# Embedding attention on one core: 68 row tiles move from ScalarE's queue to GpSimd's gathers, and the last nine steps stand in another order

## The chip, the core and the metric

The kernel runs on one core of a Trainium2 chip. A core has a matrix engine (TensorE, PE in the profile, with its weight loads shown apart as PEld), a vector engine (VectorE, DVE), an activation engine (ScalarE, ACT), a programmable engine (GpSimd, POOL) and a queue engine (SyncE, SP). The engines run side by side and wait for each other by semaphores. The metric is the device time of one execution in microseconds (us); before the change the median of three runs is 11062.63 us, between 11062.41 and 11062.69.

## What is computed

For each of 16384 users, 69 rows of a table of 100001 rows of 96 floats are fetched, and one more row, q, for the label. Each of the 69 rows is weighed by a small network that sees it beside q; ten windows sum the weighed rows; a last network of three layers turns the sums and q into one number. Cut to what matters:

```python
u = emb[batch_user]                      # 16384 x 69 x 96
ql = emb[batch_label[:, 0]]              # 16384 x 96
z = concatenate([q, u, q - u, q * u], axis=-1)
h = dice(z @ W1 + b1, a1)                # 64 wide
att = (h @ W2 + b2) @ W3 + b3
pre = where(batch_user < ITEM_NUM, u * att, 0.0)
pooled = einsum('gf,bfe->bge', window, pre)
x = concatenate([pooled, ql], axis=-1)
h = dice(bn(x @ Wf1 + bf1), af1)         # 200 wide
h = dice(bn(h @ Wf2 + bf2), af2)         # 80 wide
out = h @ Wf3 + bf3
# dice(x, a) = (a * (1 - p) + p) * x, with p = sigmoid(x)
```

## The kernel before

**Tiles.** The users are cut into 32 blocks of 512. A chunk is one of the 69 fields of one block: 512 rows of the table, in four tiles of 128 rows, one row to a partition. There are 32 x 69 = 2208 chunks, numbered c, and so 8832 tiles. Two chunks make a step, so there are 1104 steps, numbered i from 0 to 1103.

**How a tile arrives.** Nearly all tiles come by a gather (L256): one GpSimd instruction with 128 row numbers, which fetches 128 rows. 132 tiles come in another way, always the last of a chunk's four. Their rows are fetched one by one into a ring of eight buffers by plain DMAs, 128 to a tile (L294). Of these tiles 64 are fetched by SyncE's queue (`SP_CHUNKS`, one in every 17 steps) and 68 by ScalarE's (`ACT_CHUNKS`, one in every 16 steps, eight rows in each step below 1088). For these tiles there is no gather, and PE waits for the ring's semaphore in its place (`wait_for_single`).

**A step.** `fetch(i)` issues the gathers of step i and, on PE, the eight transposes (L318) that put the rows into columns; VectorE copies each chunk's 96 x 512 out (uT, L369) and makes its product with q (quT, L370). Two steps later `hidden` multiplies both by the weights of the first layer (ph, L377 and L379) and ScalarE takes the sigmoid (y, L381); `gate` finishes the dice with ScalarE (L386) and VectorE (L387). One step later `attend` makes the weight of each row (pa, L394) and VectorE multiplies the rows by it (pre, L396). One more step later `top1` multiplies the weighed rows of both chunks by the first layer of the last network, with the window sum folded into its weights V, and adds into two accumulators of 100 x 512 (p1, L407), which gather over all 69 fields of a block.

**The end of a block.** When a block's last field is in, `top1_gates`, `top2` and `top3` finish it (L415 to L447), spread over the next steps. The last block has nothing behind it. There the old kernel leaves its steady order for the last six steps (`CLOSE = 6`): each part follows the step before it more closely, and then `top1_gates`, `top2` and `top3_last` run one after the other on whole 512 columns. `store` writes the first 31 blocks' results, `top3_last` the last block's.

**What sets the order.** The program is put down by hand: a plan lists for each step what is to be recorded, and each engine runs its own instructions strictly in the order in which they were recorded. PE and VectorE do all their work in one line each, GpSimd nothing but gathers after the first microseconds.

Of the kernel before, what the change touches and what calls it, by code (L numbers as in the profile page):

```python
# [23 lines left out]
DH = D1 // 2  # L24

BLK = 512
NBLK = B // BLK
NQ = BLK // P
NT = F * NQ
NCOL = NT + NQ  # L30
NPAIR = NBLK * F // 2
S_DICE = float(1.0 / np.sqrt(1.0 + 1e-9))
S_BN = float(1.0 / np.sqrt(1.0 + 1e-5))
# [3 lines left out]

NUT, NQUT = 8, 6

CLOSE = 6  # L40

NV = 4
PER_BANK = 512 // F
# [8 lines left out]
ACT_ROWS = 8  # L52
ACT_FIRST = 4
ACT_GROUP = 3
ACT_AHEAD = 5
ACT_CHUNKS = [2 * ((s + 1) * P // ACT_ROWS + ACT_AHEAD) for s in range(68)]
ACT_RING = 4
SINGLES = SP_CHUNKS + ACT_CHUNKS
NSB = (len(SINGLES) + P - 1) // P
# [4 lines left out]
def chunk_of(c):  # L64
    return divmod(c, F)
# [49 lines left out]
def rec_kernel(  # L115
# [13 lines left out]
    nc = tc.nc  # L129
# [5 lines left out]
    ypool = ctx.enter_context(tc.tile_pool(name="ypool", bufs=3))  # L135
    ppool = ctx.enter_context(tc.tile_pool(name="ppool", bufs=6))
    bpool = ctx.enter_context(tc.tile_pool(name="bpool", bufs=2))
    xpool = ctx.enter_context(tc.tile_pool(name="xpool", bufs=1))
# [46 lines left out]
    for i in range(2):  # L185
        t = const.tile([E + 1, BLK], F32, name=f"qT{i}")
# [18 lines left out]
    wf2 = FAR.of(wf, "Wf2").rearrange("e (k n) -> e k n", n=D2)  # L205
    wf3 = FAR.of(wf, "Wf3")
    bf1c = [FAR.of(wf, "bf1")[:, i : i + 1] for i in range(2)]
    af1c = [FAR.of(wf, "af1")[:, i : i + 1] for i in range(2)]
    bf2c = FAR.of(wf, "bf2")
    af2c = FAR.of(wf, "af2")  # L210
    bf3c = FAR.of(wf, "bf3")
    res = const.tile([P, NBLK * NQ], F32, name="res")

    def dice_weights(b, a, name):

        sb, sa, sna = (const.tile(list(b.shape), F32, name=f"{name}_{k}") for k in range(3))
# [17 lines left out]
    ps_h = ctx.enter_context(tc.tile_pool(name="ps_h", bufs=2, space=PSUM))  # L234
    ps_x = ctx.enter_context(tc.tile_pool(name="ps_x", bufs=2, space=PSUM))
# [3 lines left out]
    V = const.tile([E, F, D1], F32, name="V")  # L239
# [23 lines left out]
    def call(f, *args):  # L263
        return lambda: f(*args)
# [3 lines left out]
    class Singles:  # L268
# [19 lines left out]
        def fetch(self, s, start, stop):  # L288

            b, k = self.buffers[s % len(self.buffers)], s % NSEM  # L290
            for r in range(start, stop):
                if r % self.group == 0:
                    self.load(s, r)
                d = self.engine.dma_start(  # L294
                    out=ring[r : r + 1, b], in_=row_bytes[:, bass.ds(self.values[r], ROW_BYTES)]
                ).then_inc(self.sems[k], 16)
                tc.no_tile_sem_insts.add(d.ins.name)
                tc.declare_no_dep(d.ins, group=f"ring{b}", reason="a buffer's readers have waited for its rows")
                fresh.setdefault(b, []).append(d.ins)
            if stop == P:  # L300
                for ins in fresh.pop(b):
                    tc.add_to_no_dep_group(f"ring{b}", ins)
                self.given[k] += 16 * P
                places[self.chunks[s]] = b, self.sems[k], self.given[k]
# [3 lines left out]
    def single(c, t):  # L308
        return places.get(c) if t == SLOT else None
# [41 lines left out]
            if k < m  # L351
        ]

    def fetch(i, between=None):

        u = upool.tile([P, 8, E], F32, tag="u", name=f"u{i}")
        for j in range(2):
            if j == 1 and between:
                between()
            c = 2 * i + j  # L360
            n, k = chunk_of(c)
            ptr = ps_tr.tile([E, BLK], F32, tag="tr", name=f"ptr{c}")
            for t in range(NQ):
                if single(c, t):
                    wait_for_single(c, t)
                else:
                    gather(rows, u[:, 4 * j + t, :], ids[n][:, 4 * k + t : 4 * k + t + 1])
                read_rows(nc.tensor.transpose, ptr[:, t * P : (t + 1) * P], u, c, t, ident)
            nc.vector.tensor_copy(uTs[c % NUT][0:E], ptr)  # L369
            nc.vector.tensor_tensor(quTs[c % NQUT][0:E], ptr, qTs[n % 2][0:E], ALU.mult)  # L370
# [27 lines left out]
    def top1(c):  # L398

        n, k = chunk_of(c)  # L400
        if k == 0:
            p1s[n] = [ps_p.tile([DH, BLK], F32, tag=f"p{h}", name=f"p1_{n}_{h}") for h in range(2)]
            for h, p in enumerate(p1s[n]):
                nc.tensor.matmul(p, wq[:, h * DH : (h + 1) * DH], qTs[n % 2][0:E], start=True, stop=False)  # L404
        pre = pres.pop(c)
        for h, p in enumerate(p1s[n]):
            nc.tensor.matmul(p, V[:, k, h * DH : (h + 1) * DH], pre, start=False, stop=(k == F - 1))  # L407

    def top1_gates(n):

        x1s[n] = xpool.tile([DH, 2, BLK], F32, tag="x1", name=f"x1_{n}")
        gs = [xpool.tile([DH, BLK], F32, tag=f"g{h}", name=f"g1_{n}_{h}") for h in range(2)]

        def first(h):
            nc.scalar.activation(gs[h], p1s[n][h], AF.Sigmoid, bias=dice1[h][0], scale=S_BN * S_DICE)  # L415

        def second(h):
            _, sa, sna = dice1[h]
            nc.scalar.activation(gs[h], gs[h], AF.Identity, bias=sa, scale=sna)
            nc.vector.scalar_tensor_tensor(x1s[n][:, h, :], p1s[n][h], bf1c[h], gs[h], ALU.add, ALU.mult)  # L420

        return [call(f, h) for f in (first, second) for h in range(2)]

    def top2(n):
        x2 = xpool.tile([D2, BLK], F32, tag="x2", name=f"x2_{n}")
        g2 = xpool.tile([DH, BLK], F32, tag="g0", name=f"g2_{n}")[0:D2]
        p2 = ps_x.tile([D2, BLK], F32, tag="x", name=f"p2_{n}")
        for i in range(2):
            nc.tensor.matmul(p2, wf2[:, i, :], x1s[n][:, i, :], start=(i == 0), stop=(i == 1))  # L429
        x2s[n] = x2  # L430
        sb, sa, sna = dice2

        def first():
            nc.scalar.activation(g2, p2, AF.Sigmoid, bias=sb, scale=S_BN * S_DICE)  # L434

        def second():
            nc.scalar.activation(g2, g2, AF.Identity, bias=sa, scale=sna)  # L437
            nc.vector.scalar_tensor_tensor(x2, p2, bf2c, g2, ALU.add, ALU.mult)  # L438

        return [first, second]  # L440
# [13 lines left out]
        nc.vector.tensor_copy(r, p4)  # L454
        nc.sync.dma_start(out=out[n0 * P : n1 * P].rearrange("(m p) o -> m (p o)", p=P), in_=r)

    def top3_last(n):
        x2 = x2s.pop(n)
        p3 = ps_x.tile([1, BLK], F32, tag="x", name="p3_last")
        nc.tensor.matmul(p3, wf3, x2, start=True, stop=True)  # L460
        r = ypool.tile([P, BLK], F32, tag="y", name="r_last")[0:1]
        nc.vector.tensor_scalar(r, p3, bf3c[0:1], None, ALU.add)
        nc.sync.dma_start(out=out[n * BLK :].rearrange("p o -> o p"), in_=r)

    pres, p1s, x1s, x2s, qs, phs, ys = ({} for _ in range(7))
# [3 lines left out]
    def at(step, *work):  # L469
        plan.setdefault(step, []).extend(work)  # L470

    by_sync = Singles("sp", nc.sync, mybir.EngineType.SP, SP_CHUNKS, 0, range(SP_RING), 32)
    for s, m in enumerate(SP_CHUNKS):
# [5 lines left out]
        mybir.EngineType.Activation,  # L479
        ACT_CHUNKS,  # L480
        len(SP_CHUNKS),
# [11 lines left out]

    c = NPAIR - CLOSE
    last = NPAIR - 1
# [3 lines left out]
    def tops(step, chunks):  # L499
        for m in chunks:  # L500
            at(step, call(top1, m))
            n, k = chunk_of(m)
            if k == F - 1:
                gates[step], tops2[step + 1], tops3[step + 2] = n, n, n
# [43 lines left out]
    def both(k):  # L548
        return [2 * k, 2 * k + 1]

    at(c, call(hide, c - 2), call(attends, c - 3))
    tops(c, late + both(c - 4))
    at(c, call(fetch, c, call(hide, c - 1)))
    at(c + 1, call(attends, c - 2))
    tops(c + 1, both(c - 3))
    at(c + 1, call(attends, c - 1))
    tops(c + 1, both(c - 2))
    at(c + 1, call(fetch, c + 1, call(hide, c)))
    for i in range(c + 2, NPAIR):
        tops(i, both(i - 3))  # L560
        at(i, call(attends, i - 2), call(fetch, i, call(hide, i - 1)))
    i = NPAIR
    tops(i, both(i - 3))
    at(i, call(hide, last), call(attends, i - 2))
    tops(i, both(i - 2))
    at(i, call(store, 0, (NBLK - 1) * NQ), call(attends, last))
    tops(i, both(last))

    def finish():
        n = NBLK - 1  # L570
        for job in top1_gates(n):
            job()
        for job in top2(n):
            job()
        top3_last(n)

    at(i, finish)

    for n in range(NBLK):
        first = n * F // 2  # L580
# [86 lines left out]
```

## Time and profile before

| | us |
|---|---|
| median of three runs | 11062.63 |
| the profiled execution | 11061.57 |
| its span in the trace, first to last instruction | 11059.8 |
| PE busy | 9442.5 |
| VectorE busy | 5179.0 |
| ScalarE busy | 1950.3 |
| GpSimd busy | 8332.2 |

The page of a profile gives for each engine its busy time and share, then groups of instructions by line with their count, mean duration and the idle time ahead of them, and what ended that idle time. "Issue" stands for idle time in which the engine waited for nothing that the profile shows. Times in the timeline are counted from the span's first instruction. The clock that was granted to PE is 0.940 of full speed on average.

### The profile page before, as it was taken

The page shows a single profiled execution, that of the slowest core. Times are in us where ns is not written, and L with a number is a line of the kernel's source. Part 1 is how long each engine was busy: PE and PEld are TensorE (multiplying, and loading weights), DVE is VectorE, ACT ScalarE, POOL GpSimd, SP SyncE. Part 2 cuts the span into 40 slices and gives each one's busy share as a digit, 9 for nine tenths or more (in the row PEclk, how much of TensorE's full clock was granted, in tenths as well). Part 3 has the DMA queues.
Part 4 walks back from the last instruction along what each step waited for, and adds up shares of the span by engine and source line. Part 5 has one row for each costly group of instructions (what it writes and reads, how often), then busy time and mean ns, then how long its engine had stood idle before and what let it go on. Part 6 is the DMA issues. An engine that isn't in the chain of part 4 may idle for free.

```text
span 11059.8 us, 124851 instructions
## 1 busy us (share of the span) xinstructions
PE 9442.5 (85%) x32079; PEld 3481.7 (31%) x32079; DVE 5179.0 (47%) x7995; ACT 1950.3 (18%) x2866; POOL 8332.2 (75%) x8834
## 2 busy tenths in 40 slices
PE   8888888888888888888888888888888888888888
PEld 4333333333333333333333333333333333333332
DVE  4444444444444444444444444444444444444444
ACT  1111111111111111111111111111111111111111
POOL 7777777777777777777777777777777777777776
PEclk9999999999999999999999999999999999999999
DMA  2222222222222222222222222222222222222221
GB/s 55 41 42 42 41 41 41 43 41 41 41 41 43 41 41 41 41 43 41 41 41 41 43 41 41 41 41 43 41 41 41 41 43 41 41 41 41 40 40 36
DMA packets 319006, 456.86 MB, mean 41 GB/s; under 512 B 175253, under 2 KB 175889, under 8 KB 318162
## 3 DMA queue, kind: packets, MB, share of 16 engines
q0 software_dynamic: 282496, 434.48, 19.8%
q1 hardware_dynamic: 18386, 11.02, 0.4%
q10 hardware_dynamic: 17408, 3.38, 0.2%
q8 instruction: 259, 4.24, 0.2%
q14 instruction: 457, 3.74, 0.1%
HBM read 448.18 MB, written 0.07 MB: 41 GB/s over the span
## 4 chain that ended last, share of the span: by engine, by line
POOL 45%; PE 23%; issue 21%; DMA 11%; ACT 0%; POOLq 0%; DVE 0%; ACTq 0%; DVEq 0%
POOL u L256 44%; DMA u<-in_rows,ids 10%; PE p L407 10%; PE ph L377 4%; PE ph L379 4%; PE pa L394 3%; PE ptr L318 2%; POOL q L256 1%; PE pc L339 0%; PE p L429 0%; PE p L404 0%; ACT g L437 0%; ACT g L434 0%; PE p L446 0%; ACT uT L349 0%
## 5 line engine op out<-in xcount | busy, mean ns | idle before, releaser
L256 POOL DMA_INDIRECT u<-in_rows,ids x8700 | 8210.6, 944 | 2653.0 <-issue 2478.3
L407 PE MATMUL p<-pre,V 96*100 96x512 f32 x8832 | 4059.1, 602 | 2.3 <-DVE pre L396 2.3
L318 PE MATMUL ptr<-ident,u 128*96 128x128 f32 x8700 | 1623.5, 287 | 1543.8 <-DMA u<-in_rows,ids 1513.5
L369 DVE COPY uT<-ptr 96x512 f32<-96x512 f32 x2208 | 1510.8, 684 | 2756.3 <-PE ptr L318 2746.3
L396 DVE SCALAR_TENSOR_TENSOR pre<-pa,bb,uT 96x512 f32<-96x512 f32 x2208 | 1550.7, 742 | 2120.8 <-PE pa L394 2120.8
L407 PEld LDWEIGHTS p<-pre,V 96*100 96x100 f32 x8832 | 1387.6, 167 | 2647.1 <-issue 2643.1
L381 ACT ACTIVATE y<-ph 128x512 f32<-128x512 f32 x1104 | 659.2, 597 | 7389.9 <-PE ph L379 7372.2
L318 PEld LDWEIGHTS ptr<-ident,u 128*96 128x96 f32 x8700 | 1032.5, 127 | 2639.7 <-DMA u<-in_rows,ids 1967.6
L370 DVE TENSOR_TENSOR quT<-ptr,qT 96x512 f32<-96x512 f32 x2208 | 1493.5, 676 | 0.0
L377 PE MATMUL ph<-uT,AW 128*64 128x512 f32 x4416 | 1416.4, 714 | 47.1 <-ACT uT L349 47.1
L379 PE MATMUL ph<-quT,BW 128*64 128x512 f32 x4416 | 1377.7, 697 | 0.0
L394 PE MATMUL pa<-y,vrep 64*96 64x512 f32 x4416 | 1297.1, 666 | 0.0
L386 ACT ACTIVATE y<-y,wn,na1c 128x512 f32<-128x512 f32 x1104 | 898.3, 814 | 1398.6 <-issue 850.1
L387 DVE TENSOR_TENSOR y<-ph,y 128x512 f32<-128x512 f32 x1104 | 751.8, 681 | 587.1 <-ACT y L386 587.1
L394 PEld LDWEIGHTS pa<-y,vrep 64*96 64x96 f32 x4416 | 296.1, 171 | 1087.5 <-issue 593.1
L379 PEld LDWEIGHTS ph<-quT,BW 128*64 128x64 f32 x4416 | 373.3, 158 | 778.6 <-issue 775.1
L377 PEld LDWEIGHTS ph<-uT,AW 128*64 128x64 f32 x4416 | 243.3, 146 | 263.5 <-issue 108.4
L349 ACT COPY uT<-cT 32x512 f32<-32x512 f32 x256 | 155.1, 611 | 29.5 <-DVE cT L342 17.0
L256 POOL DMA_INDIRECT q<-in_emb,ids x128 | 121.0, 945 | 40.7 <-issue 38.7
L438 DVE SCALAR_TENSOR_TENSOR x<-p,wf,g 80x512 f32<-80x512 f32 x32 | 23.9, 747 | 222.2 <-ACT g L437 222.2
L349 ACT COPY quT<-cT 32x512 f32<-32x512 f32 x192 | 116.8, 608 | 1.1 <-DVE cT L342 1.1
L339 PE MATMUL pc<-qT,Cq 97*32 97x512 f32 x128 | 84.7, 798 | 0.8 <-DVE qT L333 0.8
(60 smaller groups left out, 720.7 us busy)
## 6 DMA issues: line engine op xcount, KB each, us to landing
ring<-in_rows ACTq DMA_DIRECT2D x8704, 0.4 KB
u<-in_rows,ids POOLq DMA_INDIRECT x8700
ring<-in_rows SPq DMA_DIRECT2D x8192, 0.4 KB
ids<-in_idx SPq DMA_DIRECT2D x8, 560.0 KB, 3.8
wv<-in_fields SPq DMA_DIRECT2D x1, 2434.5 KB, 12.0
q<-in_emb,ids POOLq DMA_INDIRECT x128
wn<-in_near SPq DMA_DIRECT2D x1, 226.0 KB, 3.2
wf<-in_far SPq DMA_DIRECT2D x1, 184.0 KB, 3.3
```

The costliest lines, as they stand in the source:

```text
L256: nc.gpsimd.indirect_dma_start(out=dst, out_offset=None, in_=table, in_offset=bass.IndirectOffsetOnAxis(ap=index, axis=0),)
L318: ins = op(out, ring[:, at[0]].bitcast(F32) if at else u[:, 4 * (c % 2) + t, :], other, **how)
L369: nc.vector.tensor_copy(uTs[c % NUT][0:E], ptr)
L370: nc.vector.tensor_tensor(quTs[c % NQUT][0:E], ptr, qTs[n % 2][0:E], ALU.mult)
L377: nc.tensor.matmul(p, AW, uTs[c % NUT], start=True, stop=False)
L379: nc.tensor.matmul(p, BW, quTs[c % NQUT], start=False, stop=True)
L381: nc.scalar.activation(y, ph, AF.Sigmoid, scale=S_DICE)
L386: nc.scalar.activation(ys[i], ys[i], AF.Identity, bias=a1c, scale=na1c)
L387: nc.vector.tensor_mul(ys[i], phs.pop(i), ys[i])
L394: nc.tensor.matmul(pa, vrep[at], ys[i][at], start=True, stop=True)
L396: nc.vector.scalar_tensor_tensor(pres[c], pa, bb[0:E], uTs[c % NUT][0:E], ALU.add, ALU.mult)
L407: nc.tensor.matmul(p, V[:, k, h * DH : (h + 1) * DH], pre, start=False, stop=(k == F - 1))
```

## The change

Three things are edited.

First, `ACT_CHUNKS` becomes empty. ScalarE fetches no rows; the 68 tiles that it brought are gathered by GpSimd like nearly all others, and the 64 of SyncE stay.

Second, the last nine steps (`CLOSE = 9`) are in another order. `fetch` takes a table of work that is recorded between its transposes. From the fifth of these steps on, PE does `hidden` of the step before, `top1` of the step before that and `attends` of the step before between the transposes of one step.

Third, the end of the last block is done in two halves of 256 columns: its last two chunks' `top1` (`top1_last`), its gates, and its second and third layer (`finish`). One of the two scalings of a gate moves from ScalarE to VectorE.

```diff
-CLOSE = 6
+CLOSE = 9
+HALVES = slice(0, BLK // 2), slice(BLK // 2, BLK)
-ACT_CHUNKS = [2 * ((s + 1) * P // ACT_ROWS + ACT_AHEAD) for s in range(68)]
+ACT_CHUNKS = [2 * ((s + 1) * P // ACT_ROWS + ACT_AHEAD) for s in range(0)]
...
-    def fetch(i, between=None):
+    def fetch(i, between={}):
...
-            if j == 1 and between:
-                between()
...
             for t in range(NQ):
+                for work in between.get((j, t), ()):
+                    work()
...
+    def top1_last(n):
+        for s in HALVES:
+            for k in (F - 2, F - 1):
+                for h, p in enumerate(p1s[n]):
+                    weights = V[:, k, h * DH : (h + 1) * DH]
+                    nc.tensor.matmul(p[:, s], weights, pres[n * F + k][:, s], start=False, stop=(k == F - 1 and s is HALVES[1]))
...
-    def top3_last(n):
...
+    def finish():
...
+        for s in HALVES:
+            for h in range(2):
+                nc.scalar.activation(
+                    g1[h][:, s], p1s[n][h][:, s], AF.Sigmoid, bias=dice1[h][0], scale=S_BN * S_DICE
+                )
+            nc.scalar.activation(g1[0][:, s], g1[0][:, s], AF.Identity, bias=dice1[0][1], scale=dice1[0][2])
+            nc.vector.tensor_scalar(g1[1][:, s], g1[1][:, s], dice1[1][2], dice1[1][1], ALU.mult, ALU.add)
+            for h in (1, 0):
+                nc.vector.scalar_tensor_tensor(
+                    x1[:, h, s], p1s[n][h][:, s], bf1c[h], g1[h][:, s], ALU.add, ALU.mult
+                )
+        for s, p in zip(HALVES, p2):
+            for h in (1, 0):
+                nc.tensor.matmul(p, wf2[:, h, :], x1[:, h, s], start=(h == 1), stop=(h == 0))
+            nc.scalar.activation(g2[:, s], p, AF.Sigmoid, bias=sb, scale=S_BN * S_DICE)
+            nc.vector.tensor_scalar(g2[:, s], g2[:, s], sna, sa, ALU.mult, ALU.add)
+            nc.vector.scalar_tensor_tensor(x2[:, s], p, bf2c, g2[:, s], ALU.add, ALU.mult)
+        for s, p in zip(HALVES, p3):
+            nc.tensor.matmul(p, wf3, x2[:, s], start=True, stop=True)
+            nc.vector.tensor_scalar(r[:, s], p, bf3c[0:1], None, ALU.add)
         nc.sync.dma_start(out=out[n * BLK :].rearrange("p o -> o p"), in_=r)
...
-    for i in range(c + 2, NPAIR):
+    for i in range(c + 2, c + 5):
         tops(i, both(i - 3))
-        at(i, call(attends, i - 2), call(fetch, i, call(hide, i - 1)))
+        at(i, call(attends, i - 2), call(fetch, i, {(1, 0): [call(hide, i - 1)]}))
...
-    i = NPAIR
+    i = c + 5
     tops(i, both(i - 3))
-    at(i, call(hide, last), call(attends, i - 2))
-    tops(i, both(i - 2))
-    at(i, call(store, 0, (NBLK - 1) * NQ), call(attends, last))
-    tops(i, both(last))
...
+    at(i, call(attends, i - 2))
+    for i in range(c + 5, NPAIR):
+        between = {
+            (0, 2): [call(hide, i - 1)],
+            (0, 3): [call(top1, 2 * i - 4)],
+            (1, 0): [call(top1, 2 * i - 3)],
+            (1, 2): [call(attends, i - 1)],
+        }
+        at(i, call(fetch, i, between))
+    at(last, call(store, 0, (NBLK - 1) * NQ))
+    at(NPAIR, call(top1, 2 * last - 2), call(hide, last), call(top1, 2 * last - 1))
+    at(NPAIR, call(attends, last), call(top1_last, NBLK - 1), finish)
```

What this does to each engine's own line of instructions is shown at three places. The first is GpSimd in steps 20 to 26, where u with its step's number is the tile that a gather writes and x8 means that eight gathers follow each other. Before:

```order
L256 DMA u20_3041<-in_rows,ids0_76 128x96 x8
...
L256 DMA u21_3098<-in_rows,ids0_76 128x96 x7
L256 DMA u22_3150<-in_rows,ids0_76 128x96 x8
L256 DMA u23_3202<-in_rows,ids0_76 128x96 x8
L256 DMA u24_3325<-in_rows,ids0_76 128x96 x8
L256 DMA u25_3377<-in_rows,ids0_76 128x96 x7
```

And now:

```order
L258 DMA u20_2483<-in_rows,ids0_76 128x96 x8
...
L258 DMA u21_2532<-in_rows,ids0_76 128x96 x8
L258 DMA u22_2576<-in_rows,ids0_76 128x96 x8
L258 DMA u23_2620<-in_rows,ids0_76 128x96 x8
L258 DMA u24_2670<-in_rows,ids0_76 128x96 x8
L258 DMA u25_2714<-in_rows,ids0_76 128x96 x7
```

Step 21 held the first of ScalarE's tiles and now has its eighth gather; step 25 holds one of SyncE's and keeps seven. It is the same at 67 other steps.

The second place is PE from the last four transposes (ptr2207) to the last chunks' weighed rows (pre2206, pre2207); p1 is an accumulator, ph, pa and p4 are the products named above and the store's transpose. Before, with rows left out at each mark:

```order
L318 MATMUL ptr2207_102032<-ident_88,u1103_102011 96x128 x4
...
L377 MATMUL ph1103_102047<-uT6_110,AW_96 64x512
...
L394 MATMUL pa2204_102056<-y1102_102028,vrep_129 96x512
...
L407 MATMUL p1_31_0_100395<-pre2204_102058,V_172 100x512
...
L394 MATMUL pa2206_102073<-y1103_102052,vrep_129 96x512
L394 MATMUL pa2207_102077<-y1103_102052,vrep_129 96x512
L407 MATMUL p1_31_0_100395<-pre2206_102075,V_172 100x512
```

And now:

```order
L396 MATMUL pa2204_75657<-y1102_75638,vrep_129 96x512
L396 MATMUL pa2205_75661<-y1102_75638,vrep_129 96x512
L320 MATMUL ptr2207_75650<-ident_88,u1103_75627 96x128 x2
L462 MATMUL p4_0_75671<-ident_88,res_131 124x128
L409 MATMUL p1_31_0_74314<-pre2204_75659,V_172 100x512
...
L379 MATMUL ph1103_75678<-uT6_110,AW_96 64x512
...
L409 MATMUL p1_31_0_74314<-pre2205_75663,V_172 100x512
...
L396 MATMUL pa2206_75689<-y1103_75683,vrep_129 96x512
L396 MATMUL pa2207_75693<-y1103_75683,vrep_129 96x512
L417 MATMUL p1_31_0_74314<-pre2206_75691,V_172 100x256
```

The products pa of the step before the last have moved ahead of the last two transposes, and of its p1 products one chunk stands ahead of ph of the last step and one behind it; before, ph of the last step stood ahead of all of them, behind two chunks' p1 products of the step before that.

The third place is ScalarE in the gates of the last block, with the semaphore that each instruction waits for (g1 is a gate of one of the two accumulators, g2 that of the second layer):

```order
L480 ACTIVATE g1_last_0_75706<-p1_31_0_74314,dice1_0_0_132 100x256 [waits PE_49]
L480 ACTIVATE g1_last_1_75707<-p1_31_1_74315,dice1_1_0_138 100x256 [waits PE_49]
L483 ACTIVATE g1_last_0_75706<-g1_last_0_75706,dice1_0_1_133,dice1_0_2_134 100x256 [waits Activation_49]
L480 ACTIVATE g1_last_0_75706<-p1_31_0_74314,dice1_0_0_132 100x256 [waits DVE_49]
L480 ACTIVATE g1_last_1_75707<-p1_31_1_74315,dice1_1_0_138 100x256
L483 ACTIVATE g1_last_0_75706<-g1_last_0_75706,dice1_0_1_133,dice1_0_2_134 100x256 [waits Activation_49]
L492 ACTIVATE g2_last_75709<-p2_last_0_75711,dice2_0_144 80x256 [waits PE_49]
L492 ACTIVATE g2_last_75709<-p2_last_1_75712,dice2_0_144 80x256 [waits PE_49]
```

Before there were six activations of 512 columns in this place and none waited for VectorE. Now the first of the second half (the fourth row) waits for VectorE, which reads the first half of the same gate tile, and neither of the second half's sigmoids has a wait for PE of its own.

More of the change, by code (lines that the diff above doesn't have):

```diff
@@ L455, in store @@
         nc.sync.dma_start(out=out[n0 * P : n1 * P].rearrange("(m p) o -> m (p o)", p=P), in_=r)
-    def top3_last(n):
-        x2 = x2s.pop(n)
-        p3 = ps_x.tile([1, BLK], F32, tag="x", name="p3_last")
-        nc.tensor.matmul(p3, wf3, x2, start=True, stop=True)
-        r = ypool.tile([P, BLK], F32, tag="y", name="r_last")[0:1]
-        nc.vector.tensor_scalar(r, p3, bf3c[0:1], None, ALU.add)
+    def finish():
+        n = NBLK - 1
+        x1 = xpool.tile([DH, 2, BLK], F32, tag="x1", name="x1_last")
+        g1 = [xpool.tile([DH, BLK], F32, tag=f"g{h}", name=f"g1_last_{h}") for h in range(2)]
+        x2 = xpool.tile([D2, BLK], F32, tag="x2", name="x2_last")
+        g2 = ypool.tile([P, BLK], F32, tag="y", name="g2_last")[0:D2]
+        r = ypool.tile([P, BLK], F32, tag="y", name="r_last")[0:1]
+        p2 = [ps_x.tile([D2, BLK // 2], F32, tag="x", name=f"p2_last_{k}") for k in range(2)]
+        p3 = [ps_h.tile([1, BLK // 2], F32, tag="h", name=f"p3_last_{k}") for k in range(2)]
+        sb, sa, sna = dice2
+        for s in HALVES:
[18 more added lines that the diff above has]
+            nc.vector.tensor_scalar(r[:, s], p, bf3c[0:1], None, ALU.add)
         nc.sync.dma_start(out=out[n * BLK :].rearrange("p o -> o p"), in_=r)
@@ L552, in rec_kernel @@
     tops(c, late + both(c - 4))
-    at(c, call(fetch, c, call(hide, c - 1)))
+    at(c, call(fetch, c, {(1, 0): [call(hide, c - 1)]}))
     at(c + 1, call(attends, c - 2))
@@ L557, in rec_kernel @@
     tops(c + 1, both(c - 2))
-    at(c + 1, call(fetch, c + 1, call(hide, c)))
-    for i in range(c + 2, NPAIR):
+    at(c + 1, call(fetch, c + 1, {(1, 0): [call(hide, c)]}))
+    for i in range(c + 2, c + 5):
         tops(i, both(i - 3))
-        at(i, call(attends, i - 2), call(fetch, i, call(hide, i - 1)))
-    i = NPAIR
+        at(i, call(attends, i - 2), call(fetch, i, {(1, 0): [call(hide, i - 1)]}))
+    i = c + 5
     tops(i, both(i - 3))
-    at(i, call(hide, last), call(attends, i - 2))
-    tops(i, both(i - 2))
-    at(i, call(store, 0, (NBLK - 1) * NQ), call(attends, last))
-    tops(i, both(last))
[L569 to L577, printed above, removed]
+    at(i, call(attends, i - 2))
[10 more added lines that the diff above has]
+    at(NPAIR, call(attends, last), call(top1_last, NBLK - 1), finish)
     for n in range(NBLK):
```

## The prediction

> **What bounds the kernel now.** I read the page first, for the span, the engines, the chain and the largest groups.
>
> ```profile
> span 11059.8 us, 124851 instructions
> PE 9442.5 (85%) x32079; PEld 3481.7 (31%) x32079; DVE 5179.0 (47%) x7995; ACT 1950.3 (18%) x2866; POOL 8332.2 (75%) x8834
> ...
> q0 software_dynamic: 282496, 434.48, 19.8%
> ...
> POOL 45%; PE 23%; issue 21%; DMA 11%; ACT 0%; POOLq 0%; DVE 0%; ACTq 0%; DVEq 0%
> ...
> L256 POOL DMA_INDIRECT u<-in_rows,ids x8700 | 8210.6, 944 | 2653.0 <-issue 2478.3
> ...
> L318 PE MATMUL ptr<-ident,u 128*96 128x128 f32 x8700 | 1623.5, 287 | 1543.8 <-DMA u<-in_rows,ids 1513.5
> ...
> L256 POOL DMA_INDIRECT q<-in_emb,ids x128 | 121.0, 945 | 40.7 <-issue 38.7
> ...
> ring<-in_rows ACTq DMA_DIRECT2D x8704, 0.4 KB
> ```
>
> PE is the busiest engine by its 85%, but its transposes stand idle 1513.5 us for gathered rows, so PE is fed, not feeding. GpSimd is busy only 75%. Its 2653.0 us of idle time are the thing to read, and the view of GpSimd's waits shows what ended them.
>
> ```profile
> POOL u L256 <- issue: 2478.3, 8127, 0.3
> POOL u L256 <- DMA u<-in_rows,ids: 88.4, 290, 0.3
> POOL u L256 <- PE ptr L318: 74.4, 244, 0.3
> ...
> POOL q L256 <- DMA ids<-in_idx: 2.0, 1, 2.0
> ```
>
> The columns are total, count and longest. No gap between gathers is longer than 0.3 us, whatever is named as its end, except the 2.0 us ahead of the first. A gap of 0.30 belongs to every gather. GpSimd is therefore never held up by a buffer or by PE; it issues one gather after the other from start to end. The timeline of GpSimd and of ScalarE's queue gives the pace.
>
> ```profile
> 3.27 1.10 POOL L256 DMA_INDIRECT q<-in_emb,ids  x1 [1.95 <-DMA ids<-in_idx]
> ...
> 10864.73 1.13 ACTq L294 DMA_DIRECT2D ring<-in_rows  x4
> ...
> 10871.99 0.94 POOL L256 DMA_INDIRECT u<-in_rows,ids  x1 [0.30 <-issue]
> ...
> 11025.56 0.94 POOL L256 DMA_INDIRECT u<-in_rows,ids  x1 [0.30 <-issue]
> ```
>
> The page counts 8700 + 128 = 8828 gathers. From the first start to the last are 11022.29 us and 8827 intervals: **1.24870 us each**. ScalarE's last row fetches are at 10864.73. From 10871.99, after them, to the last gather there are 123 intervals, counted by this row of the windows (124 gathers):
>
> ```profile
> 10871.90:11026.60 154.70, 117.03 (x124) 0.97 0.20 40
> ```
>
> That is 153.57 / 123 = 1.24854 us. The pace is the same with and without ScalarE's transfers, to 0.2 ns. So the time is 3.27 us of start, 8828 gathers, and a tail behind the last.
>
> **The change: 68 more gathers.** 8832 tiles less 64 make 8768 gathers, with 128 for the labels 8896. 68 x 1.24870 = **+84.9 us**, all on the bound, since GpSimd has no idle time to hide it in. PE does not get in the way: 9442.5 us over 1104 steps are 8.55 us a step, and a step of eight gathers now always takes 8 x 1.2487 = 9.99. What ScalarE sheds, 8704 small transfers and their row-number loads, is worth nothing in itself: ScalarE is busy 18%, and what it does faster waits for GpSimd. The cover of this zero is GpSimd's pace; a bound for what the lost transfers could give back is the difference of the two paces, 0.2 ns, which I widen to 0.3 ns either way, since both come from rows rounded to 10 ns: 8896 x 0.3 ns = 2.7 us. The smaller load of row numbers at the start stands on SP's queue behind the one that the first gather waits for, so it moves nothing. The gathers' waits for free buffers stay as short as they are: the order of GpSimd's line is unchanged, and no buffer is used longer than before.
>
> **The change: the tail.** The timeline of the old tail, PE's weight loads left out:
>
> ```profile
> 11028.10 0.31 PE L318 MATMUL ptr<-ident,u 128*96 128x128 f32 x1 [0.92 <-DMA u<-in_rows,ids]
> 11028.25 3.60 PE L407 MATMUL p<-pre,V 96*100 96x512 f32 x8
> ...
> 11029.06 0.68 DVE L370 TENSOR_TENSOR quT<-ptr,qT 96x512 f32<-96x512 f32 x1
> 11031.78 1.08 PE L377 MATMUL ph<-uT,AW 128*64 128x512 f32 x4
> 11032.69 1.03 PE L379 MATMUL ph<-quT,BW 128*64 128x512 f32 x4
> ...
> 11035.26 0.69 DVE L387 TENSOR_TENSOR y<-ph,y 128x512 f32<-128x512 f32 x1 [5.53 <-ACT y L386]
> ...
> 11036.66 5.37 PE L407 MATMUL p<-pre,V 96*100 96x512 f32 x8 [1.92 <-DVE pre L396]
> ...
> 11042.08 1.55 PE L394 MATMUL pa<-y,vrep 64*96 64x512 f32 x4
> ...
> 11043.21 1.41 DVE L396 SCALAR_TENSOR_TENSOR pre<-pa,bb,uT 96x512 f32<-96x512 f32 x2 [0.73 <-PE pa L394]
> 11044.01 3.68 PE L407 MATMUL p<-pre,V 96*100 96x512 f32 x8 [0.39 <-DVE pre L396]
> 11046.87 0.69 ACT L415 ACTIVATE g<-p,dice 100x512 f32<-100x512 f32 x1 [11.64 <-PE p L407]
> ...
> 11049.95 2.60 PE L429 MATMUL p<-x,wf 100*80 100x512 f32 x4 [2.27 <-DVE x L420]
> 11052.59 0.68 ACT L434 ACTIVATE g<-p,dice 80x512 f32<-80x512 f32 x1 [2.77 <-PE p L429]
> 11053.31 0.81 ACT L437 ACTIVATE g<-g,dice,dice 80x512 f32<-80x512 f32 x1
> 11054.16 0.75 DVE L438 SCALAR_TENSOR_TENSOR x<-p,wf,g 80x512 f32<-80x512 f32 x1 [3.55 <-ACT g L437]
> 11054.96 1.86 PE L460 MATMUL p_last<-x,wf 80*1 80x512 f32 x2 [2.40 <-DVE x L438]
> 11056.86 0.74 DVE L462 TENSOR_SCALAR r_last<-p_last,wf 1x512 f32<-1x512 f32 x1 [1.96 <-PE p_last L460]
> 11057.63 0.24 SPq L463 DMA_DIRECT2D out<-r_last  x1
> ```
>
> I count from the last transpose, T = 11028.10; the result is sent off at T + 29.53, and the rest to the span's end, 2.2 us, stays. The old tail has two p1 groups ahead of the last step's weights: 3.60 us at T + 0.15, and 5.37 us at T + 8.56, behind which the last pa waits until 11042.08 although y was ready at 11035.95. Now the new chain, in order:
>
> 1. The last copies (uT, quT) end at T + 1.64 before. Now two pre stand ahead of them on VectorE, and pa for these ahead of the last transposes on PE. PE's spare time in a step (9.99 less 8.55) lets it reach the last rows about when they land; I allow 0.2 us.
> 2. PE does the store's transpose and one chunk's p1, half of 3.60, and is free at T + 2.1; then ph, from 11031.78 to 11033.72, takes 1.94: T + 4.0.
> 3. Sigmoid, scaling and product to y end at 11035.95, 2.23 after ph: T + 6.2. The other p1 chunk (1.80) lies on PE beneath it.
> 4. pa to the end of the second pre: 11042.08 to 11044.62, 2.54: T + 8.8.
> 5. The last p1: the same columns in halves. The row with 3.68 starts 0.61 ahead of the end of pre: T + 11.9.
> 6. The gates in halves. These sizes are not in the trace, so I scale by these rows of the groups by shape:
>
> ```profile
> L253 ACT COPY V<-pV 96x483 f32<-96x483 f32 x14 | 8.5, 606 | 40.1 <-PE pV L250 40.1
> ...
> L253 ACT COPY V<-pV 96x69 f32<-96x69 f32 x2 | 0.6, 278 | 1.1 <-PE pV L250 1.1
> ```
>
> 414 columns cost 0.328 us, so 256 fewer save 0.20: a sigmoid takes 0.49 in place of 0.69, a scaling 0.61 in place of 0.81, and a VectorE product, by the same step, some 0.52 in place of 0.75. By the order, the first half's sigmoids wait for PE and the second half's have no wait for PE of their own; so I take it that the first wait covers both halves' products, and nothing overlaps with PE. The second half also waits for VectorE's product of the first. Queued behind that waiting sigmoid are the other one, the scaling and both activations of the second layer: ScalarE stands still until VectorE is done. Each half is then 2 x 0.49 + 0.61 + 0.52 + 0.1 of hand-overs = 2.2: T + 16.3.
> 7. Second and third layer of the second half: product 0.6 (half of the 0.9 a 512-column product takes in the row of 3.60 for four, and some latency), sigmoid 0.49, scaling on VectorE 0.29, product 0.52, last product 0.6, bias 0.5, five hand-overs of 0.05: 3.25, T + 19.5. The scaling is by this timeline row of the start, the nearest in size, from memory to memory; its other bound is the 0.74 of the last bias.
>
> ```profile
> 3.32 0.29 DVE L153 TENSOR_SCALAR offsets<-offsets 128x256 int32<-128x256 int32 x1 [1.23 <-DMA offsets<-in_single_rows]
> ```
>
> 29.5 - 19.5 = **-10.0 us** at PE's full rate. The old results' store goes out earlier, at about T + 4, and the last bias, which waits for its landing, comes 15 us later. Bounds: if half the columns cost half the time, steps 6 and 7 are 3.0 and 2.1, and the gain 12.5. If they cost as much as whole ones (6.1 and 5.1) and PE runs step 5 at half its rate (3.4 more, as bounded by a full halving of the row of 3.68), the end is T + 26.5 and the gain 3.0. I stay near the scaled rows.
>
> On PE's rate: the same eight products took 5.37 us after an idle time of 1.92 and 3.68 after one of 0.39, and the lone product at 11054.96, after 2.40 idle, took 1.86 where 0.9 is usual. The small products between the gates also come after gaps of one to two us. At half the rate the two that lie on the chain take 0.45 more each, 0.9 in all; I add 0.5 of it, between that and nothing.
>
> The Trainium skill, "TensorE: Matmul & The Clock Gate", section "Part 1: The HAM clock gate (the "warmup" mystery)", has the clock halved only after an idle window of about 3.4 us. By it these shorter gaps would leave the rate full and the sum 0.5 lower; the row with 5.37 after 1.92 of idleness speaks against that, and the row decides.
>
> **Sum.** 11061.57 (profiled) + 84.9 - 10.0 = 11136.5. The median before stands 1.06 above the profiled execution, so 11137.5, and with the 0.5 for slow small products **11138 us**, 0.68% slower.
>
> **Rivals.**
> - The tail gains nothing: with p1, ph and pa between the last transposes PE comes late to the last rows, and slow products eat the rest. For it speaks that the last two transposes now stand behind two chunks' p1 and two pa of the same step; against it the 0.92 us for which PE waits at T, and the two p1 groups that leave the chain. 11062.63 + 84.9 = 11147.5. Chance 0.05.
> - The gathers are not the bound, but the 16 DMA engines or PE, and 68 tiles that change the queue cost nothing: 11062.63 - 10.0 = 11052.6, within the 0.2% (22 us) that a measurement can tell from no change. PE's 23% of the chain speaks for it; the constant pace, the 19.8% that the gather queue takes of the DMA engines and the absent waits of GpSimd speak against it. The Trainium skill, "DMA: Bandwidth & Descriptors", section "Issuing engines are not separate DMA queues", is on this side: it says that issuing from several engines saves only issue time, usually small beside the transfer. Here the issue, 1.25 us, is the whole bound. Chance 0.03.
> - The other sign: ScalarE's transfers hold GpSimd back, and without 8704 of them the gap of 0.30 between gathers shrinks. It decides from 75 / 8896 = 8.4 ns a gather; with 15 ns, a twentieth of the gap, 133 us go and 11005 is left. Against it: the pace after 10871.99, without such transfers, is only 0.2 ns lower. Chance 0.03.
> - My forecast has the rest, 0.89. That the change does not do what it says is out: the order shows the eighth gather.
>
> **Range.** A gain of the tail between 3.0 and 12.5 gives 11144.5 to 11135.0, the pace 2.7 either way: 11132.3 to 11147.2. I give **11132.5 to 11147**, which leaves out the other rivals. Faster by over 0.2%: 0.03; within it 0.03; slower 0.94.
>
> **What would show it.** x8768 at L258 and a pace of 1.2487; a last gather that starts near 11110.5; no longest wait of GpSimd over 0.3. In the tail, the result sent 18 to 21 us behind the last transpose; the second half's first sigmoid starting behind VectorE's first product. I am wrong if the pace moves by more than a nanosecond, if GpSimd shows waits, or if PE comes more than 1 us late to the last rows.

## The result, and the profile after

The changed kernel takes 11137.69 us (median of four, 11137.29 to 11139.20) where the kernel before takes 11062.54: 75.15 us or 0.68% longer, ratio 1.0068 with a 95% interval of 1.0056 to 1.0081. The profiled execution is the longest of the four, 11139.20; its span is 11137.4. On the page after, the lines that answer to those of before are the engines, the chain and the gathers:

```profile
span 11137.4 us, 107206 instructions
PE 9505.4 (85%) x32093; PEld 3491.0 (31%) x32093; DVE 5172.4 (46%) x8003; ACT 1950.2 (18%) x2868; POOL 8396.6 (75%) x8902
...
POOL 43%; PE 24%; issue 19%; DMA 12%; ACT 0%; DVE 0%; POOLq 0%; DVEq 0%
...
L258 POOL DMA_INDIRECT u<-in_rows,ids x8768 | 8274.9, 944 | 2672.7 <-issue 2464.8
```

There are 68 gathers more, each as long as before, and nearly all else on the page stands still. The shares of the chain hardly move, although what the change adds lies in GpSimd's line: a share does not tell what bounds a kernel, the waits of the engine do. GpSimd's waits after (total, count, longest), and the first and the last gather in its timeline:

```profile
POOL u L258 <- issue: 2464.8, 8086, 0.3
POOL u L258 <- DMA u<-in_rows,ids: 120.4, 395, 0.3
POOL u L258 <- PE ptr L320: 76.2, 250, 0.3
```

```profile
3.27 1.12 POOL L258 DMA_INDIRECT q<-in_emb,ids  x1 [1.95 <-DMA ids<-in_idx]
...
11109.67 0.94 POOL L258 DMA_INDIRECT u<-in_rows,ids  x1 [0.30 <-issue]
```

No wait between gathers is longer than 0.3 us. 8896 gathers give 8895 intervals in 11106.40 us, 1.24861 us each, 0.09 ns less than before. The last gather starts 84.11 us later than it did. What follows is the tail; its timeline after, with PE's rows of the last step first:

```profile
11105.89 1.93 PE L381 MATMUL ph<-quT,BW 128*64 128x512 f32 x4
...
11107.99 2.48 PE L409 MATMUL p<-pre,V 96*100 96x512 f32 x4
...
11113.48 0.42 PE L320 MATMUL ptr<-ident,u 128*96 128x128 f32 x2
...
11114.39 0.33 PE L462 MATMUL p<-ident,res 128*124 128x128 f32 x1 [0.48 <-DVE pre L398]
...
11116.36 1.08 PE L379 MATMUL ph<-uT,AW 128*64 128x512 f32 x4
...
11121.73 1.41 DVE L398 SCALAR_TENSOR_TENSOR pre<-pa,bb,uT 96x512 f32<-96x512 f32 x2 [1.19 <-PE pa L396]
11122.53 3.70 PE L417 MATMUL p<-pre,V 96*100 96x256 f32 x16 [0.83 <-DVE pre L398]
11125.83 0.91 ACT L480 ACTIVATE g_last<-p,dice 100x256 f32<-100x256 f32 x2 [6.02 <-PE p L417]
...
11127.29 0.88 DVE L486 SCALAR_TENSOR_TENSOR x_last<-p,wf,g_last 100x256 f32<-100x256 f32 x2
...
11128.20 0.84 ACT L480 ACTIVATE g_last<-p,dice 100x256 f32<-100x256 f32 x2 [0.97 <-DVE x_last L486]
...
11130.06 2.00 PE L491 MATMUL p_last<-x_last,wf 100*80 100x256 f32 x4 [1.14 <-DVE x_last L486]
...
11135.22 0.24 SPq L498 DMA_DIRECT2D out<-r_last  x1
```

The old tail sent the result 32.07 us after the last gather's start (11057.63 - 11025.56), the new one 25.55 us (11135.22 - 11109.67): 6.5 us are given back. 84.1 - 6.5 is the 77.6 us by which the two profiled executions differ; the medians differ by 75.2.

Two things show in these rows. PE is late: by the old kernel's distance of 2.54 us from a gather's start to its transpose, the last rows land at 11112.21, but the last two transposes start at 11113.48, since ph (1.93 where the old tail has 1.03) and a p1 chunk (2.48 where half of 3.60 is usual) ran slowly. And the halves of the gates do not overlap: the second half's sigmoids start 0.97 us after ScalarE was free, behind VectorE.

The slow products ran at half the clock. In a row of the windows view stand a stretch of time, its length, PE's busy time with the count of its instructions, the clock granted to PE, and the DMA engines' share and GB/s. The first row is the stretch from that ph on, the second the last products of the second layer; in the fourth run below the clock is 1.00 from the same ph on:

```profile
11105.90:11108.90 3.00, 3.00 (x9) 0.50 0.18 39
11130.00:11132.10 2.10, 2.04 (x5) 0.50 0.00 0
```

```profile
11067.70:11070.70 3.00, 3.00 (x13) 1.00 0.25 50
```

The runs below from the fifth on went to other chips, on which the kernel before itself takes 13224 to 13323 us at a mean granted clock near 0.84 (0.94 in the case), and none of their times is compared with this case.

### The profile page after: what moved, and what is told of

The parts are those of the page before. It is cut to its first block, busy times and chain, and to the rows that moved or that the text cites. A ratio compares the mean times of both kernels' runs of the same rounds, so it can differ in the third digit from the quotient of the medians.

```text
span 11137.4 us, 107206 instructions
## 1 busy us (share of the span) xinstructions
PE 9505.4 (85%) x32093; PEld 3491.0 (31%) x32093; DVE 5172.4 (46%) x8003; ACT 1950.2 (18%) x2868; POOL 8396.6 (75%) x8902
## 4 chain that ended last, share of the span: by engine, by line
POOL 43%; PE 24%; issue 19%; DMA 12%; ACT 0%; DVE 0%; POOLq 0%; DVEq 0%
POOL u L258 42%; DMA u<-in_rows,ids 12%; PE p L409 10%; PE ph L379 4%; PE ph L381 4%; PE pa L396 3%; PE ptr L320 2%; POOL q L258 1%; PE p L406 0%; PE pc L341 0%; PE p L439 0%; ACT g L447 0%; PE p L456 0%; ACT uT L351 0%; ACT g L444 0%
```

## The experiments

**One part at a time.** Four runs on one chip share 22 executions of the kernel before, with a median of 11066.70 us (11061.75 to 11068.32). The first moves the 68 tiles alone, in the kernel before:

```diff
-ACT_CHUNKS = [2 * ((s + 1) * P // ACT_ROWS + ACT_AHEAD) for s in range(68)]
+ACT_CHUNKS = [2 * ((s + 1) * P // ACT_ROWS + ACT_AHEAD) for s in range(0)]
```

> Old order of the last steps, old whole-width end; only the 68 tiles go from ScalarE to GpSimd. Theory A (each tile costs one gather at GpSimd's pace, the new tail gives 9 us back): 11062.5 + 84.1 = 11146.6 us, between 11145 and 11148. Theory B (the new tail gives nothing, and the gathers cost only the 75 us that the whole change cost): 11137.7.

Measured: 11150.57 us, ratio 1.0076 (1.0059 to 1.0092). That is 83.9 above the kernel before on this chip, where theory A had 84.1 and theory B 75. The expected times of these four runs were reckoned from the times of the result (11062.5 for the kernel before), and the kernel before takes 4.2 us more here; all four measured times lie 4 to 5 us above what theory A gave, and outside its range where it gave one, so it is the distance from the kernel before, or between runs, that is compared. The timeline of the first run, from the last gather on:

```profile
11113.81 0.95 POOL L256 DMA_INDIRECT u<-in_rows,ids  x1 [0.30 <-issue]
```

```profile
11116.49 5.29 PE L407 MATMUL p<-pre,V 96*100 96x512 f32 x8
...
11126.60 5.37 PE L407 MATMUL p<-pre,V 96*100 96x512 f32 x8 [1.92 <-DVE pre L396]
...
11147.60 0.24 SPq L463 DMA_DIRECT2D out<-r_last  x1
```

The old order keeps its long tail, 33.8 us from the last gather's start, with both p1 groups slow (5.29 and 5.37 us; in the kernel before the first took 3.60). So the gathers cost their full price, and what the change gives back comes from the tail.

The second run is the other part, the changed kernel with ScalarE's tiles back:

```diff
-ACT_CHUNKS = [2 * ((s + 1) * P // ACT_ROWS + ACT_AHEAD) for s in range(0)]
+ACT_CHUNKS = [2 * ((s + 1) * P // ACT_ROWS + ACT_AHEAD) for s in range(68)]
```

> New order of the last nine steps and halves; ScalarE keeps its 68 tiles. Theory A: 11062.5 - 9.0 = 11053.5 us, between 11052 and 11056. Theory B (the new tail gives nothing): 11062.5.

Measured: 11057.88 us (ten executions, 11055.53 to 11059.35), 8.8 below the kernel before; theory A had 9.0 and theory B none. The ratio, 0.9992 (0.9983 to 1.0002), does not leave out that there is no difference, so the time alone would not settle it, though all ten executions lie below the 22 of the kernel before. The timeline does. Here PE in the last step, then the last gather and the sending of the result:

```profile
11023.02 1.82 PE L381 MATMUL ph<-quT,BW 128*64 128x512 f32 x4
...
11029.83 0.42 PE L320 MATMUL ptr<-ident,u 128*96 128x128 f32 x2
```

```profile
11025.98 0.94 POOL L258 DMA_INDIRECT u<-in_rows,ids  x1 [0.30 <-issue]
...
11051.56 0.24 SPq L498 DMA_DIRECT2D out<-r_last  x1
```

From the last gather's start to the sending are 25.58 us, as in the changed kernel, and 6.5 less than in the kernel before. The other 2.3 of the 8.8 us are within what the pace of the gathers varies by from one execution to the next (last section). PE is late here too: the transposes start 3.85 us after the last gather's start, where 2.54 is in time, again behind a slow ph. This version has the lowest time of those that ran on this chip.

The third run takes the halves out of the second, so that the order of the last nine steps stands alone:

```diff
-    at(NPAIR, call(attends, last), call(top1_last, NBLK - 1), finish)
+    at(NPAIR, call(attends, last), call(top1, 2 * last), call(top1, 2 * last + 1), finish)
...
+    def finish():
+        n = NBLK - 1
+        for job in top1_gates(n):
+            job()
+        for job in top2(n):
+            job()
+        top3_last(n)
```

> As the tail alone, but the last block's last products, gates and layers on whole 512 columns as before; ScalarE keeps its 68 tiles. Theory A with the prediction's own steps: the order brings the end of the last p1 product from T + 19.6 to T + 11.9, 7.7 of the 10 us, so 11062.5 - 7 = 11055.5, and the halves about 2. Rival: the halves bring most, 11060.

Measured: 11060.29 us (ten executions), 6.4 below the kernel before, ratio 0.9995 (0.9985 to 1.0004), so this time alone settles nothing either. It is near the rival's 11060, but that was a gain of 2.5 us on the 11062.5 it was reckoned from; a gain of 6.4 is nearer to theory A's 7. In its timeline:

```profile
11029.64 0.94 POOL L258 DMA_INDIRECT u<-in_rows,ids  x1 [0.30 <-issue]
```

```profile
11040.97 3.68 PE L409 MATMUL p<-pre,V 96*100 96x512 f32 x8 [0.83 <-DVE pre L398]
...
11054.55 0.24 SPq L465 DMA_DIRECT2D out<-r_last  x1
```

The last p1 product ends 12.5 us after the last rows landed (11044.65, with 11032.18 for the landing), where the old tail has 19.6: the order gives 7.1 us. From there to the sending are 9.9 us, as in the old tail (11047.69 to 11057.63).

The fourth run keeps the halves and gives half of the tiles back to ScalarE:

```diff
-ACT_CHUNKS = [2 * ((s + 1) * P // ACT_ROWS + ACT_AHEAD) for s in range(0)]
+ACT_CHUNKS = [2 * ((s + 1) * P // ACT_ROWS + ACT_AHEAD) for s in range(34)]
```

> The changed kernel, but ScalarE keeps the first 34 of its 68 tiles. Theory A (in proportion to the number of gathers): 34 x 1.2486 = 42.5 less than the changed kernel, 11095.2 us, between 11094 and 11097. Rival (the time depends on whether ScalarE transfers rows at all, not on how many gathers there are): at the changed kernel's 11137.7 or at the 11053.5 of the tail alone.

Measured: 11100.01 us, ratio 1.0031 (1.0019 to 1.0042). It is 42.1 us above the tail alone, where 34 gathers make 42.5. The time follows the number of gathers, not whether ScalarE transfers rows at all. The timeline of its tail has PE in time:

```profile
11071.44 0.95 POOL L258 DMA_INDIRECT u<-in_rows,ids  x1 [0.30 <-issue]
```

```profile
11067.70 1.03 PE L381 MATMUL ph<-quT,BW 128*64 128x512 f32 x4
```

```profile
11082.75 3.70 PE L417 MATMUL p<-pre,V 96*100 96x256 f32 x16 [0.83 <-DVE pre L398]
...
11090.28 2.00 PE L491 MATMUL p_last<-x_last,wf 100*80 100x256 f32 x4 [1.14 <-DVE x_last L486]
...
11095.43 0.24 SPq L498 DMA_DIRECT2D out<-r_last  x1
```

The p1 products end 12.5 us after the landing at 11073.98, as in the third run, and 9.0 us later the result is sent. Between the two runs the halves are worth 0.9 us, the order 7.1 against the old tail; together the result goes out 21.45 us after the landing, where the old tail has 29.53. The medians of the second and third run differ by 2.4 us, but they cannot size the halves: in the two profiled executions the last gathers, with the same work in front of them, start 3.7 us apart.

**What the rest of the runs say.** They were made on the chips on which the kernel before takes 13224 us and more. What GpSimd does there is shown by its waits in a run of the changed kernel with another order in the last gates:

```profile
POOL u L258 <- issue: 2340.6, 7668, 0.7
POOL u L258 <- remote: 1358.1, 386, 5.4
POOL u L258 <- PE ptr L320: 501.5, 170, 29.9
```

GpSimd waits up to 29.9 us at a time for PE, and much of the rest is put down to releasers that the trace does not show; in the case no wait between gathers is over 0.3. What holds the engines up there was not settled. Two runs test the rival that ScalarE's transfers hold GpSimd back, both with this edit, which leaves out the 68 tiles:

```diff
+                if c in SKIPPED and t == SLOT:
+                    nc.tensor.transpose(ptr[:, t * P : (t + 1) * P], zero, ident)
+                    continue
```

> The changed kernel with ScalarE's 68 tiles neither gathered nor fetched: PE transposes a tile of zeros in their place, so these rows' part of the result is left out. 8828 gathers as before, no transfers of ScalarE. Theory A (only the number of gathers counts): as the tail alone, 8.8 us below the kernel before. Rival (ScalarE's 8704 transfers hold GpSimd or PE back in themselves): more than 3 us below the tail alone, so over 12 us below the kernel before, with a shorter mean interval between gathers.

> The changed kernel with ScalarE's 68 tiles neither gathered nor fetched, once more beside a kernel before that takes its usual time: PE transposes a tile of zeros in their place, so these rows' part of the result is left out. 8828 gathers, no transfers of ScalarE. Theory A (only the number of gathers counts): as the tail alone, 8.8 us below the kernel before, within 3. Rival (ScalarE's 8704 transfers hold GpSimd back): over 12 us below the kernel before, with a mean interval between gathers more than 0.4 ns shorter.

Measured: 13117.74 beside 13224.03, ratio 0.9918 (0.9897 to 0.9939), and 13117.60 beside 13227.58, ratio 0.9912 (0.9895 to 0.9928). There the kernel with the new tail and without the transfers takes 106 and 110 us less. By its number that is the rival, but GpSimd is held by waits there that the case does not have, so it says nothing on the case, and an interval between gathers there is no measure of their pace. In the case the rival falls by the traces: the interval is 1.24870 in the kernel before and 1.24861 in the changed one.

Two more runs concern the wait in the last gates, with the changed kernel's activations all recorded ahead of VectorE's work on them:

```diff
             nc.scalar.activation(g1[0][:, s], g1[0][:, s], AF.Identity, bias=dice1[0][1], scale=dice1[0][2])
+        for s in HALVES:
             nc.vector.tensor_scalar(g1[1][:, s], g1[1][:, s], dice1[1][2], dice1[1][1], ALU.mult, ALU.add)
```

> The changed kernel with all six activations of the last gates recorded ahead of VectorE's work on them, so that none of them waits for VectorE; VectorE's first product then waits for ScalarE's fifth activation. Theory A (the order between the two engines on one accumulator only changes sides): from the end of the last p1 product to the sending of the result 8.7 us, where the changed kernel has 9.0. Rival (ScalarE's wait of 0.97 us was a cost of its own): 8.0.

> The changed kernel with all six activations of the last gates recorded ahead of VectorE's work on them, so that none waits for VectorE; VectorE's first product then waits for ScalarE's fifth activation. Theory A (the order between two engines on one accumulator only changes sides): from the end of the last p1 product to the sending of the result 8.7 us, where the changed kernel has 9.0. Rival (ScalarE's wait of 0.97 us was a cost of its own): 8.0.

They took 13183.26 and 13226.23 us, one execution each, 41 and 1 us below the kernel before on their chips: there the 68 gathers do not cost what they cost in the case. What they show is the order of the end. The first, in its timeline:

```profile
13166.92 3.70 PE L417 MATMUL p<-pre,V 96*100 96x256 f32 x16 [0.83 <-DVE pre L398]
...
13171.17 0.41 DVE L485 TENSOR_SCALAR g_last<-g_last,dice,dice 100x256 f32<-100x256 f32 x1 [3.64 <-ACT g_last L480]
...
13171.53 0.82 ACT L480 ACTIVATE g_last<-p,dice 100x256 f32<-100x256 f32 x2
...
13172.39 0.88 DVE L487 SCALAR_TENSOR_TENSOR x_last<-p,wf,g_last 100x256 f32<-100x256 f32 x2 [0.81 <-ACT g_last L480]
...
13172.92 3.23 PE L492 MATMUL p_last<-x_last,wf 100*80 100x256 f32 x8 [2.30 <-DVE x_last L487]
...
13179.31 0.24 SPq L499 DMA_DIRECT2D out<-r_last  x1
```

ScalarE's second half no longer waits, and VectorE's first product now waits 0.81 us for it. From the end of p1 (13170.62) to the sending are 8.69 us, as theory A had it: the wait changed sides, and in this one execution the end comes 0.3 us sooner than in the changed kernel's trace. In the second run the same stretch took 7.36 us, which is below the rival's 8.0, but for another reason, in this row of its timeline:

```profile
13217.21 2.32 PE L492 MATMUL p_last<-x_last,wf 100*80 100x256 f32 x8 [2.30 <-DVE x_last L487]
```

The same products took 3.23 us in the first run, and the products of the last layer 1.01 us twice, where the second has 0.59. The clock granted to PE was 1.00 from 13217.2 to 13219.5 in the second run and 0.66 from 13172.9 to 13176.1 in the first. So PE's clock at that moment moves the end of the kernel by more than the wait does.

The order hangs on the accumulator p1 that both engines read, not on the gate tile: VectorE's scaling, which touches the gate tile alone, starts at 13171.17 and does not wait for the second half's sigmoids, which end at 13172.35; the product behind it, which reads the accumulator too, starts only then.

**Further tiles off GpSimd.** If gathers are the bound, more of them should go to SyncE's queue. Its waits in the kernel before (total, count, longest):

```profile
SPq L294 <- PE ptr L318: 6872.0, 59, 123.0
```

Between two of its tiles it stands some 116 us (6872.0 / 59) for the buffer that PE has still to read. The edits are counts and spacing: 180 tiles of SyncE, one in 6 steps and begun 18 steps ahead, with ScalarE's 68; the same with 136 of ScalarE, at twice the rows a step; and 134 of SyncE, one in 8 steps, with ScalarE's 68, this one twice. SyncE's part of the last:

```diff
-SP_STEPS = 17
+SP_STEPS = 8
-SP_CHUNKS = [2 * (int(SP_STEPS * s) + SP_FIRST) + 1 for s in range(64)]
+SP_CHUNKS = [2 * (int(SP_STEPS * s) + SP_FIRST) + 1 for s in range(134)]
```

> The tail alone, with SyncE bringing 180 tiles in place of 64 (one in every 6 steps, begun 18 steps ahead) and ScalarE its 68: 8712 gathers. Theory A (in proportion to the gathers): 116 x 1.249 = 144.9 below the tail alone, 153.7 below the kernel before, near 10913 us. Rival (PE, which is 85% busy, or SyncE's queue becomes the bound): less than 110 below, with waits of PE for the ring's semaphore or with no more waits of PE for gathers.

> As the run with 180 tiles of SyncE, and ScalarE brings 136 in place of 68, 16 rows in each step: 8644 gathers. Theory A: 184 x 1.249 = 229.8 below the tail alone, 238.6 below the kernel before, near 10828 us. Rival (ScalarE's longer issue delays the sigmoids, or PE becomes the bound): between 10830 and 10913, or above the run with 180 tiles.

> The tail alone, with SyncE bringing 134 tiles in place of 64 (one in every 8 steps, 80 us, of which a tile takes SyncE's queue 48) and ScalarE its 68: 8758 gathers. Theory A (in proportion to the gathers): 70 x 1.249 = 87.4 below the tail alone, 96.2 below the kernel before, near 10966 us. Rival (PE, busy 85%, or SyncE's queue becomes the bound): less than 60 below the kernel before, with waits of PE for the ring's rows or of GpSimd for PE.

> The same kernel once more (SyncE 134 tiles, ScalarE 68, 8758 gathers), in the hope of a chip on which the kernel before takes its usual 11063 us. Theory A: 96 below the kernel before. Rival: less than 60 below it. If the kernel before takes 13220 here too, SyncE's queue is the bound as in the run before this one, and the kernel is 5 to 6% slower than the kernel before.

Measured, each beside the kernel before of its own chip: 15782.39 (ratio 1.1921, 1.1895 to 1.1947), 15868.93 (1.1993, 1.1941 to 1.2044), 13984.81 (1.0577, 1.0559 to 1.0594) and 14168.68 (1.0644, 1.0619 to 1.0669). All are far slower than theory A, as the rival has it. PE's waits in the first of them:

```profile
PE ptr L320 <- DMA ring<-in_rows: 3599.5, 166, 33.8
```

PE waits 166 times, up to 33.8 us, for tiles of the ring; at most 68 of these can be ScalarE's, so on these chips SyncE's queue does not bring its tiles in time. It also issues its rows more slowly there. Here is a stretch of SyncE's queue in the kernel before, and one in the first run with the other gates, on the chip of the run with 180 tiles:

```profile
5020.01 47.45 SPq L294 DMA_DIRECT2D ring<-in_rows  x124
```

```profile
5999.88 50.12 SPq L296 DMA_DIRECT2D ring<-in_rows  x69
```

By the first row a tile of 128 rows takes some 49 us, less than the 60 us of six steps; by this estimate 180 tiles would fit in the case. Whether they do stays open, for no run shows it.

## Why the prediction was right

- **The bound.** GpSimd's gathers one after the other was the reading, and it held: no wait over 0.3 us after either, and the time follows the number of gathers in three runs of one chip (68, 34 and none of the tiles moved).
- **The 68 gathers.** Predicted +84.9, measured 84.11 at the last gather; the run of this part alone gives 83.9, good to the few us by which the pace varies. The 0.8 between the first two is the pace, 0.09 ns x 8895, within the 0.3 ns that the prediction allowed.
- **The tail.** Predicted -10.0, with 0.5 added for slow products; the profiled execution shows -6.5. The mechanism was right: the two old p1 groups left the chain, and the gates' second half waits for VectorE. But the gain was put too high. From the landing to the sending are 23.0 us, where steps 1 to 7 end at 19.5, and three terms make up the 3.5. "I allow 0.2 us" for PE's coming late to the last rows: it came 1.3 us late, behind products at half the clock. That was named as a sign of being wrong ("more than 1 us late"), and by this sign the term was wrong; the sending, 21.7 us behind the last two transposes, is outside the named 18 to 21 too. The transpose of the store was counted as nearly free in step 2, but it needs a buffer of the pool that pa uses and waits 0.48 us for VectorE's pre, and ph with it: from these transposes to ph are 2.9 us where 1.9 were reckoned. Steps 3 to 5 hold to 0.1 us. Steps 6 and 7 came to 7.6 (8.1 with the 0.5) and take 9.0: the gates are 0.2 shorter, the layers 1.6 longer, for their products ran at the clock of 0.50. Behind its last input the second layer's product takes 1.7 us and the last one 1.0, where 0.6 each was reckoned.
- **The sum.** 11138 predicted, 11137.69 measured. The closeness is partly luck: the gain of the profiled execution is 3.0 us smaller than the forecast with its 0.5; the pace gives 0.8 of that back, the forecast added 1.1 for the median before being above its profiled execution, and the profiled execution after is itself 1.5 above its median. How the tail of the median execution looks, no trace tells.
- **The rivals.** A tail without gain falls by the runs of the parts: with the new order 12.5 us from landing to the end of p1, without it 19.6. That the gathers are hidden falls by the run of this part alone. That ScalarE's transfers hold GpSimd back needs 8.4 ns a gather; the two kernels differ by 0.09, and the six traces of the result and the first four runs by under 0.6.

## What to carry to other kernels

An engine that is busy 75% can be the whole bound: read the longest wait of each engine, not its share. If an engine issues without waits, the price of moving work to it is the distance from start to start, gap included, and nothing hides it. A reordered tail is worth measuring piece by piece in the trace, since its microseconds are about as many as the scatter of the whole time (6.6 us over the 22 executions of the kernel before).

## What had not been expected of the hardware

The pace of the gathers is not the same in all executions: by the first and last starts of the gathers it was 1.24875 us in the second run and 1.24917 in the third, which have the same gathers and the same transfers of ScalarE, on one chip, and 1.24908 without the transfers in the first. The largest of these differences is 3.7 us over 8827 intervals. It goes with no part of the change.

PE's granted clock drops to 0.50 for some microseconds in places that shift from run to run: the same four products of ph took 1.03, 1.82 and 1.93 us in the fourth run, the second run and the changed kernel, at clocks of 1.00, 0.55 and 0.50. The length of the idle time just ahead does not tell where: the second layer's products ran at 0.66 and at 1.00 in the two runs with the other gates, both after 2.30 us of idle time, and the drop in the changed kernel came after waits of no more than 0.83 us in that step. What sets it was not found. In a kernel that ends on PE this moves the end by 1 to 2 us.
